# A causal mask moved from TensorE to GpSimd in an attention and mixture-of-experts kernel

## The chip, the cores and the metric

The kernel runs on one core of a Trainium2 chip. The metric is device time in microseconds (us) of one execution. Engines are named as in the profile: PE is TensorE's matmul, PEld its weight load, DVE is VectorE, ACT is ScalarE, POOL is GpSimd, SP is the engine that issues most DMAs. L679 means line 679 of the kernel before.

## The reference, cut to what matters

The input x has 8 sequences of 1024 tokens with 512 features. The first half is attention with 16 heads of 32 features on the normalized x. Queries and keys are the cosine and sine of angles, 64 numbers per head. The part that the change touches is the causal mask:

```python
scores = jnp.einsum('bqhd,bkhd->bhqk', Q, K) / scale
causal = jnp.triu(jnp.ones((S, S), dtype=bool), k=1)
scores = jnp.where(causal, -jnp.inf, scores)
attn = jax.nn.softmax(scores, axis=-1)
out = jnp.einsum('bhqk,bkhd->bqhd', attn, V).reshape(B, S, D)
```

The second half is a mixture of experts: a router picks two of 8 experts for each token, each expert takes at most 160 tokens of a sequence, and tokens go through two matrix products (512 to 2048 to 512). Both halves are added to x.

## The kernel before

**Stages.** The first 1275 us or so are attention; the rest is the experts, which the change leaves alone. Attention runs in 32 *chunks*: chunk n is sequence n // 4 and features 128 (n % 4) onwards, that is four heads. A chunk has two *pairs* of heads, and each pair two *halves* of 512 queries. Only what is not wholly masked is computed: half 0 has 3 score tiles, half 1 has 7. The last three tiles of each half hold the keys on the diagonal; the helper `tiles_of` makes them out of one key block with 512 queries, two blocks with 384 and 128 queries side by side, and one block with 256. Call them tiles a, b and c of the half: a has one diagonal square of 128 keys by 128 queries, b two, c one. So a half has 4 such squares, a chunk 16, the kernel 512.

**A score tile.** `scores` (L670) multiplies keys by queries into PSUM (L679): for each of the two heads of the pair one matmul that uses 64 of the 128 rows of the array, so two run side by side, and each shows as two passes in the trace. In tiles a, b and c four bf16 matmuls follow into the same PSUM tile (L693), which add a large negative number where a key is later than its query; `keys_b` and `later_b` are the constants they multiply. Then ACT takes the exponential into the SBUF tile `e` (L699). PSUM holds three such tiles of two banks. `attend` (L713) multiplies the weights `e` by the values into `av`; DVE scales it into `av_sb` (L721). `turn` transposes `av_sb` (L215), divides by the sum of the weights (L748, L750) and puts the result into `o_p`.

**Beside it.** For the next chunks DVE and ACT make the angles of queries and keys (`qk_pre` L520, `angle` L440, squares L444, sines L447 and L589, products L450) and of the values (`v_pre` L621, L626; `v_post`). The base of an angle (position times a constant) is made once per feature chunk by `make_base` (L463 to L493) and read back later. From the fifth chunk on, the *router* of the sequence before runs in steps between these: `features` transposes two token tiles and copies them (L832), `next_rows` normalizes the next two (L807) and stores them to DRAM, `sums` multiplies by the router's weights (L869), copies the products (L874), gathers them (L852) and adds the bias into `prob` (L876). Most of these steps fall into the chunks with n % 4 == 1.

**Order.** PE, ACT, DVE and SP run in the order in which the program text issues the work; the loop over n writes this order out by hand, with generators (`some`, `with_asides`, `route_on`) that advance one tile at a time. In pair 0 the 10 score tiles come first (5, then 5 with other work between), then all its products with the values; in pair 1 the three tiles of half 0, two of half 1, then the products of half 0. A half's products therefore stand some tiles behind its exponentials. POOL is placed by a scheduler and executes what it gets in order: a few constants, the scatters of tokens to slots (L764, 16 for each sequence, each behind the one before), the fetch of the slots back (L991), the gathers of the experts (L1080), and, near the end of attention, a few subtractions of weights (L1159). Scatters of a sequence are issued together, in the last chunk of the next sequence.

Of the kernel before, what the change touches and what calls it, by code (L numbers as in the profile page):

```python
# [63 lines left out]

FIRST = 6 * P
REACH = [(0, -(-FIRST // CAP)), (FIRST // CAP, B)]

FAR = 1000.0 * math.sqrt(2 * DH) / (UNIT * UNIT)

ROOT_GUESS = float(0x5F3759DF)  # L70

# [2 lines left out]
def preln_attn_moe_kernel(  # L74
# [184 lines left out]
    nc.gpsimd.memset(ones, 1.0)  # L259

    before = own.tile([P, P], F32, name="before")


    keys_b = own.tile([P, 2, P], BF16, name="keys_b")
    nc.gpsimd.memset(keys_b, 0.0)
    later_b = own.tile([P, 2, P], BF16, name="later_b")
    e_row = own.tile([P, E], F32, name="e_row")
    e_row_low = own.tile([P, E], F32, name="e_row_low")
    dropped = own.tile([P, NTT, TOPK], F32, name="dropped")
# [12 lines left out]
    empty = own.tile([P, E * CAP // P, 2], I32, name="empty")  # L282
    nc.vector.memset(empty, 0)

    later = row2.tile([P, NCH, 2 * P], F32, name="xT", bufs=1)[:, :3, :P]

    def mask():
        for part in range(2):
            for a in range(2):
                r = slice(a * 64, (a + 1) * 64)  # L290
                nc.gpsimd.tensor_copy(later_b[r, part, :], later[r, 1 + part - a, :])
                nc.gpsimd.tensor_copy(keys_b[r, part, part * 64 : part * 64 + 64], ident[r, r])

    def rest_of_loads():

        nc.gpsimd.memset(later, 0.0)
        for i in range(3):
            nc.gpsimd.affine_select(
                out=later[:, i, :], in_=later[:, i, :], compare_op=ALU.is_ge, fill=-FAR,
                base=64 * (1 - i), pattern=[[1, P]], channel_multiplier=-1,  # L300
            )
# [153 lines left out]
    def make_base(c):  # L455
# [33 lines left out]
                )  # L489
        else:  # L490
            nc.vector.tensor_scalar(p, p, UNITS, None, ALU.mult)
            wrap(p, r)
        nc.sync.dma_start(base_d[c], p)  # L493
        bases[c] = p

# [173 lines left out]

    def scores(pair, h, es):  # L670

        for parts in tiles_of(h):
            n = sum(w for _, _, w, _ in parts)
            ps = two_banks()
            own_keys = parts[0][0] >= 4 * h
            for kb, q0, w, at in parts:
                for a in range(2):
                    r = slice(a * 64, (a + 1) * 64)
                    nc.tensor.matmul(  # L679
                        ps[:, a, at : at + w], lhsT=pair[r, 1, kb * P : (kb + 1) * P],  # L680
                        rhs=pair[r, 0, q0 : q0 + w], start=at == 0, stop=not own_keys,
                        skip_group_check=True,
                    )
            if own_keys:

                for part, w in ((0, 64), (1, P)):
                    for a in range(2):
                        r = slice(a * 64, (a + 1) * 64)
                        out_, late = ps[:, a, :w], later_b[r, part, :w]
                        if len(parts) == 2:  # L690
                            out_ = ps[:, a, :].rearrange("p (k q) -> p k q", q=P)[:, ::3, :w]
                            late = late.unsqueeze(1).to_broadcast([64, 2, w])
                        nc.tensor.matmul(  # L693
                            out_, lhsT=keys_b[r, part, :], rhs=late,
                            start=False, stop=part == 1, skip_group_check=True,
                        )

            e = ep.tile([P, 2, n], F32, name=f"e_{n}", bufs=8 if n == 512 else 2)
            nc.scalar.activation(  # L699
                e, ps[:, :, :n], AF.Exp, scale=UNIT * UNIT / math.sqrt(2 * DH)  # L700
            )
            es.append(e)
            yield

# [48 lines left out]
        )  # L753


    scatters = []
    scattered = {b: [] for b in range(B)}
    mixed = []

    def scatter(count=2 * NTT * TOPK, together=False):  # L760

        for _ in range(min(count, len(scatters))):
# [6 lines left out]
            if together:  # L769
# [6 lines left out]
                )  # L776
                for other in scattered[b]:
                    tc.declare_no_dep(ins, other, reason="rows of their own")
            scattered[b].append(ins)

    def router(b):
# [103 lines left out]
        for g in range(NTT // 2):  # L885
            xT = features(g)
            if last and g == 0:
                yield
            if g + 1 < NTT // 2:
                if not last:  # L890
                    yield
                next_rows(g)
            yield
            lg = sums(g, xT, lg)
            yield
# [442 lines left out]
    next(base0)  # L1338
    next(base1)
    rest_of_loads()  # L1340
    mask()
    first_stats(2, NTT)
    layernorm_first()
    rest(base0)
# [12 lines left out]
    for n in range(NCK):  # L1357
# [59 lines left out]
        else:  # L1417
            with_asides(5)
        rest(residual)
        for _ in range(3):  # L1420
            route_on(1)
        rest(angles)
        if begin:
# [5 lines left out]
        if late:  # L1429
            some(4, *products)  # L1430
        route_on(1)
        with_asides(5)
        if begin:
            square(v_st[0])
        for g in asides:
            rest(g)
        if n == 0:
            load_base(2)
            magnitude(inv_o)
        if late:  # L1440
            turn(1, halves1, pos)
            o_st = o_pre(n - 1, pos)
# [4 lines left out]
        if c == 3 and b > 0:  # L1447
            next(route)
            if b > 1:
                fetch_slots(b - 2)  # L1450
            if b < B - 1:
                scatter()


        some(3, *products)
        if more:
            qk_st = place[0]
            qk_sin(qk_st)
# [112 lines left out]
```

## Time and profile before

| | us |
|---|---|
| three timed runs | 3272.74, 3274.41, 3276.23 (median 3274.41) |
| the profiled execution | 3277.64 |
| its span, first to last instruction | 3275.9 |
| busy over the span: PE, DVE, ACT, POOL | 3190.8, 2255.8, 1323.3, 426.2 |
| attention, 35 to 1275: PE, DVE, ACT, POOL busy | 1205.69, 976.08, 1016.67, 169.47 |
| the bf16 matmuls of the mask (L693), 1536 of them: busy | 175.5 |

A PE matmul's row in the profile starts when the matmul is issued, and its end is modelled; matmuls overlap, so what one costs is read from the start of one to the start of the next, and not from its duration. A timeline row has its start, its length, engine, line, operation, the tiles it writes and reads, shapes, how many instructions were merged, and in brackets how long the engine was idle before and what ended that.

### The profile page before, as it was taken

How to read it: one execution, taken by the hardware profiler on the slowest of the kernel's cores; microseconds unless marked ns; L12 is line 12 of the kernel's file. 1: busy time of each engine (PE TensorE's matmuls, PEld its weight loads, DVE VectorE, ACT ScalarE, POOL GpSimd, SP SyncE). 2: the span in 40 equal slices, each digit the busy share in tenths (PEclk: the TensorE clock that was granted, in tenths of full speed). 3: DMA queues.
4: the chain of work that ended last, by engine and by line, in shares of the span. 5: the costliest groups of instructions: out<-in, count | busy, mean ns of one | idle time of the engine just before them, and what ended most of it. 6: DMA issues, size and time to landing. Idle time of an engine off the chain costs nothing.

```text
span 3275.9 us, 48751 instructions
## 1 busy us (share of the span) xinstructions
PE 3190.8 (97%) x18942; PEld 2164.6 (66%) x18942; DVE 2255.8 (69%) x4961; ACT 1323.3 (40%) x1617; POOL 426.2 (13%) x387
## 2 busy tenths in 40 slices
PE   5999999999999999999999999999999999999998
PEld 2444444444444444588688688688688688688687
DVE  8887888878788675755755855855855855855854
ACT  7888887878787874201201201201201201201201
POOL 3000202011110213311011011011011011011010
PEclk9999999999999999999999999999999999999999
DMA  5435454453645352322322322322322322322321
GB/s 162 143 97 166 133 147 139 132 155 104 181 114 158 91 162 70 114 54 73 103 46 73 103 46 73 103 47 72 103 48 71 104 48 69 106 49 69 105 42 26
DMA packets 235254, 319.74 MB, mean 98 GB/s; under 512 B 22456, under 2 KB 155280, under 8 KB 222992
## 3 DMA queue, kind: packets, MB, share of 16 engines
q1 hardware_dynamic: 211664, 273.38, 28.6%
q0 software_dynamic: 22912, 43.22, 7.4%
q8 instruction: 150, 2.46, 0.3%
q14 instruction: 80, 0.66, 0.1%
q10 hardware_dynamic: 448, 0.02, 0.0%
HBM read 187.62 MB, written 61.82 MB: 76 GB/s over the span
## 4 chain that ended last, share of the span: by engine, by line
PE 57%; DVE 0%; DMA 0%; issue 0%; POOLq 0%; POOL 0%; DVEq 0%
PE ps_p L1220 29%; PE ps_p L1175 27%; PE ps_t L1121 1%; DMA slots<-slot_d 0%; DMA out_dram<-y,slots 0%; DVE w L1053 0%; DVE w_t L1054 0%; DVE w_t L1052 0%; DVE w_t L1055 0%; POOLq L1567 0%; POOL slot_d L764 0%; POOL slots L991 0%; DVE y L1236 0%; DVE p L1257 0%; DVE p L1258 0%
## 5 line engine op out<-in xcount | busy, mean ns | idle before, releaser
L699 ACT ACTIVATE e<-ps_s 128x1024 f32<-128x1024 f32 (+1 forms) x640 | 569.7, 938 | 202.5 <-PE ps_s L679 113.6
L679 PE MATMUL ps_s<-qk 64*128 64x512 f32 (+3 forms) x3072 | 601.9, 507 | 40.3 <-DMA qk<-qk_r 12.4
L1220 PE MATMUL ps_p<-w,hid 128*128 128x256 f32 x2560 | 567.1, 379 | 0.0
L1220 PEld LDWEIGHTS ps_p<-w,hid 128*128 128x128 f32 x2560 | 484.0, 190 | 66.6 <-DVE hid L1193 0.5
L713 PE MATMUL av<-e,v 128*64 128x512 f32 (+3 forms) x3072 | 524.7, 491 | 0.0
L1220 PE MATMUL ps_p<-w_t,hid 128*128 128x256 f32 x1920 | 430.5, 379 | 2.0 <-DVE w_t L1054 2.0
L679 PEld LDWEIGHTS ps_s<-qk 64*128 64x128 f32 x3072 | 262.0, 188 | 231.4 <-issue 111.7
L1220 PEld LDWEIGHTS ps_p<-w_t,hid 128*128 128x128 f32 x1920 | 361.1, 190 | 50.1 <-DVE w_t L1054 2.8
L713 PEld LDWEIGHTS av<-e,v 128*64 128x64 f32 x3072 | 200.8, 137 | 284.7 <-issue 268.1
L1175 PE MATMUL ps_p<-xe,w 128*128 128x256 f32 (+1 forms) x1024 | 297.8, 434 | 0.0
L1175 PE MATMUL ps_p<-xe_s,t 128*128 128x256 f32 (+1 forms) x1024 | 296.9, 433 | 0.0
L1175 PE MATMUL ps_p<-xe,t 128*128 128x256 f32 (+1 forms) x1024 | 296.8, 433 | 0.0
L764 POOL DMA_INDIRECT slot_d<-token,slot x128 | 162.4, 1268 | 974.3 <-issue 627.4
L1251 ACT COPY p<-ps_p 128x256 f32<-128x256 f32 x40 | 14.7, 369 | 604.3 <-PE ps_p L1220 604.3
L1175 PEld LDWEIGHTS ps_p<-xe,t 128*128 128x128 f32 x1024 | 194.4, 190 | 80.9 <-issue 0.4
L1175 PEld LDWEIGHTS ps_p<-xe_s,t 128*128 128x128 f32 x1024 | 194.3, 190 | 80.7 <-issue 0.4
L1175 PEld LDWEIGHTS ps_p<-xe,w 128*128 128x128 f32 x1024 | 193.4, 190 | 80.8 <-DVE hid L1193 3.5
L1080 POOL DMA_INDIRECT xg<-xn_d,source x76 | 75.2, 990 | 1074.8 <-PE ps_t L1121 1064.0
L1242 POOL DMA_INDIRECT out_dram<-y,slots x80 | 126.5, 1582 | 624.1 <-DVE y L1237 624.1
L1190 ACT ACTIVATE p<-ps_p,b_t 128x256 f32<-128x256 f32 (+1 forms) x128 | 65.5, 511 | 336.2 <-PE ps_p L1175 182.1
L1207 ACT ACTIVATE hid<-hid,b_more 128x256 f32<-128x256 f32 (+1 forms) x128 | 71.8, 561 | 274.8 <-DVE hid L1206 270.0
L1194 ACT ACTIVATE hid<-hid 128x256 f32<-128x256 f32 (+1 forms) x128 | 60.1, 470 | 299.5 <-DVE hid L1193 295.3
(224 smaller groups left out, 3818.6 us busy)
## 6 DMA issues: line engine op xcount, KB each, us to landing
w<-in_L_ffn_W_dram SPq DMA_DIRECT2D x256, 256.0 KB
w<-in_L_ffn_W_dram SPq DMA_DIRECT2D x64, 512.0 KB
qk<-qk_c SPq DMA_DIRECT2D x124, 256.0 KB
qk<-qk_r SPq DMA_DIRECT2D x124, 256.0 KB
qk_base<-base_d SPq DMA_DIRECT2D x28, 1024.0 KB
xn_d<-xn SPq DMA_DIRECT2D x72, 256.0 KB
x_mid<-in_L_attn_x_dram SPq DMA_DIRECT2D x16, 1024.0 KB
out_dram<-x_mid SPq DMA_DIRECT2D x8, 2048.0 KB
```

The costliest lines, as they stand in the source:

```text
L679: nc.tensor.matmul(ps[:, a, at : at + w], lhsT=pair[r, 1, kb * P : (kb + 1) * P], rhs=pair[r, 0, q0 : q0 + w], start=at == 0, stop=not own ...
L699: nc.scalar.activation(e, ps[:, :, :n], AF.Exp, scale=UNIT * UNIT / math.sqrt(2 * DH))
L713: nc.tensor.matmul(av[a * 64 : (a + 1) * 64, q0 - 512 * h :], lhsT=vt[:, kb, 2 * pr + a, :], rhs=es[i][:, a, at : at + w], start=kb == 0, ...
L764: queued = nc.gpsimd.indirect_dma_start(out=slot_d[b], out_offset=bass.IndirectOffsetOnAxis(ap=idx, axis=0), in_=src, in_offset=None,)
L1080: ins = nc.gpsimd.indirect_dma_start(out=xg, out_offset=None, in_=xn2_d[i % 2], in_offset=bass.IndirectOffsetOnAxis(ap=source[:, e, j0 + j ...
L1121: nc.tensor.transpose(ps[:, c, :], xg[:, c * P : (c + 1) * P], ident)
L1175: nc.tensor.matmul(ps, lhsT=weights[:, k, :], rhs=rows[:, k, :], start=k == 0, stop=k == 1)
L1190: nc.scalar.activation(p1, product(b11, a11), AF.Identity, bias=b1_t[:, e * NHC + q : e * NHC + q + 1])
L1194: nc.scalar.activation(h11, h11, AF.Relu)
L1207: nc.scalar.activation(h12, h12, AF.Relu, bias=more)
L1220: nc.tensor.matmul(ps, lhsT=hs[k][:, part, cols], rhs=ws[k][weight], start=k == 0, stop=k == NHQ - 1,)
L1242: ins = nc.gpsimd.indirect_dma_start(out=out, out_offset=bass.IndirectOffsetOnAxis(ap=meta[:, e, jj[r], 0:1], axis=0), in_=ys[r], in_offse ...
```

## The change

It has four parts.

1. **The mask.** The bf16 matmuls, their constants and the code that makes them go. After the exponential of a tile a, b or c, POOL runs one `affine_select` for each diagonal square: 128 keys by 2 heads by 128 queries of `e` are kept where the query is not earlier than the key, and set to zero elsewhere. These 512 instructions are kept in program order on POOL.
2. **The scatters.** They are no longer issued together: after the last tile of each half, two of those that wait are issued, in program order, so that 16 take eight halves. Those of sequence 6 are held back for the ending, where they also were before.
3. **The router.** In group 1, `sums` comes ahead of `next_rows`, and one step of the router is issued later in the chunk, so that the group's `sums` and then its rows stand behind the values' angles.
4. **The third base.** `make_base(2)` is issued in three steps through chunk 0 rather than in one, and the small preparation of `inv_o`, by which `av_sb` is scaled, comes ahead of it.

```diff
-    keys_b = own.tile([P, 2, P], BF16, name="keys_b")
-    nc.gpsimd.memset(keys_b, 0.0)
-    later_b = own.tile([P, 2, P], BF16, name="later_b")
...
-    def mask():
-        for part in range(2):
-            for a in range(2):
-                r = slice(a * 64, (a + 1) * 64)
-                nc.gpsimd.tensor_copy(later_b[r, part, :], later[r, 1 + part - a, :])
-                nc.gpsimd.tensor_copy(keys_b[r, part, part * 64 : part * 64 + 64], ident[r, r])
...
             nc.vector.tensor_scalar(p, p, UNITS, None, ALU.mult)
-            wrap(p, r)
+            if c == 2:
+                yield
+                nc.vector.tensor_scalar(r, p, ROUNDT, ROUNDT, ALU.add, ALU.subtract)
+                yield
+                nc.vector.tensor_tensor(p, p, r, ALU.subtract)
+            else:
+                wrap(p, r)
...
-                        rhs=pair[r, 0, q0 : q0 + w], start=at == 0, stop=not own_keys,
+                        rhs=pair[r, 0, q0 : q0 + w], start=at == 0, stop=True,
                         skip_group_check=True,
                     )
-            if own_keys:
-
-                for part, w in ((0, 64), (1, P)):
-                    for a in range(2):
-                        r = slice(a * 64, (a + 1) * 64)
-                        out_, late = ps[:, a, :w], later_b[r, part, :w]
...
-                        nc.tensor.matmul(
-                            out_, lhsT=keys_b[r, part, :], rhs=late,
-                            start=False, stop=part == 1, skip_group_check=True,
-                        )
 
             e = ep.tile([P, 2, n], F32, name=f"e_{n}", bufs=8 if n == 512 else 2)
             nc.scalar.activation(
                 e, ps[:, :, :n], AF.Exp, scale=UNIT * UNIT / math.sqrt(2 * DH)
             )
+            if own_keys:
+
+                for _, _, _, at in parts:
+                    own_ = e[:, :, at : at + P]
+                    tc.keep_in_program_order(
+                        nc.gpsimd.affine_select(
+                            out=own_, in_=own_, compare_op=ALU.is_ge, fill=0.0, base=0,
+                            pattern=[[0, 2], [1, P]], channel_multiplier=-1,
+                        )
+                    )
+            if parts is tiles[-1] and not hold[0]:
+
+                scatter(2)
             es.append(e)
             yield
...
+            if g == 1 and not last:
+
+                yield
+                lg = sums(g, xT, lg)
+                yield
+                next_rows(g)
+                yield
+                continue
...
         rest(residual)
-        for _ in range(3):
+        for _ in range(2):
             route_on(1)
         rest(angles)
...
             some(4, *products)
         route_on(1)
+        route_on(1)
         with_asides(5)
...
         if n == 0:
-            load_base(2)
             magnitude(inv_o)
+            base2 = make_base(2)
+            next(base2)
...
-            if b < B - 1:
-                scatter()
+            hold[0] = b == B - 1
 
 
         some(3, *products)
+        if n == 0:
+            next(base2)
...
+        if n == 0:
+            some(NTT, *products)
+            rest(base2)
```

More of the change, by code (lines that the diff above doesn't have):

```diff
@@ L66 @@
 REACH = [(0, -(-FIRST // CAP)), (FIRST // CAP, B)]
-FAR = 1000.0 * math.sqrt(2 * DH) / (UNIT * UNIT)
 ROOT_GUESS = float(0x5F3759DF)
@@ L283, in preln_attn_moe_kernel @@
     nc.vector.memset(empty, 0)
-    later = row2.tile([P, NCH, 2 * P], F32, name="xT", bufs=1)[:, :3, :P]
-    def mask():
-        for part in range(2):
-            for a in range(2):
-                r = slice(a * 64, (a + 1) * 64)
-                nc.gpsimd.tensor_copy(later_b[r, part, :], later[r, 1 + part - a, :])
-                nc.gpsimd.tensor_copy(keys_b[r, part, part * 64 : part * 64 + 64], ident[r, r])
-    def rest_of_loads():
[L296 to L300, printed above, removed]
-            )
+    def rest_of_loads():
         nc.gpsimd.affine_select(
@@ L670, in scores @@
     def scores(pair, h, es):
-        for parts in tiles_of(h):
+        tiles = tiles_of(h)
+        for parts in tiles:
             n = sum(w for _, _, w, _ in parts)
@@ L680, in scores @@
                         ps[:, a, at : at + w], lhsT=pair[r, 1, kb * P : (kb + 1) * P],
-                        rhs=pair[r, 0, q0 : q0 + w], start=at == 0, stop=not own_keys,
+                        rhs=pair[r, 0, q0 : q0 + w], start=at == 0, stop=True,
                         skip_group_check=True,
                     )
-            if own_keys:
-                for part, w in ((0, 64), (1, P)):
-                    for a in range(2):
-                        r = slice(a * 64, (a + 1) * 64)
-                        out_, late = ps[:, a, :w], later_b[r, part, :w]
[L690 to L693, printed above, removed]
-                            out_, lhsT=keys_b[r, part, :], rhs=late,
-                            start=False, stop=part == 1, skip_group_check=True,
-                        )
             e = ep.tile([P, 2, n], F32, name=f"e_{n}", bufs=8 if n == 512 else 2)
@@ L753, in turn @@
         )
-    scatters = []
+    scatters, hold = [], [False]
     scattered = {b: [] for b in range(B)}
@@ L778, in scatter @@
                     tc.declare_no_dep(ins, other, reason="rows of their own")
+            else:
+                tc.keep_in_program_order(queued)
             scattered[b].append(ins)
@@ L1340, in preln_attn_moe_kernel @@
     rest_of_loads()
-    mask()
     first_stats(2, NTT)
```

## The prediction

> **What bounds the kernel now.** The change touches attention alone, so I took the 1240 us of it first. By stretches of one chunk each, PE is busy nearly always in an ordinary chunk, and ACT and DVE are close behind; a chunk with router steps is longer and PE has pauses in it:
>
> ```profile
> 577.78:614.17 36.39, 36.34 (x306) 17.92 (x304) 30.69 (x69) 32.14 (x33) 0.00 (x0) 1.00 0.43 116
> 686.50:731.23 44.73, 42.10 (x434) 21.12 (x436) 33.21 (x50) 34.40 (x34) 4.67 (x5) 1.00 0.68 208
> ```
>
> Columns: stretch, its length, then PE, PEld, DVE, ACT and POOL busy, clock, DMA. Busy PE could hide waiting, so next PE's timeline, start against start, over tiles a, b, c of one half:
>
> ```profile
> 607.91 0.60 PE L679 MATMUL ps_s<-qk 64*128 64x512 f32 x2
> 608.35 0.25 PE L693 MATMUL ps_s<-later_b,keys_b 64*128 64x64 bf16 x4
> 608.43 1.09 PE L679 MATMUL ps_s<-qk 64*128 64x384 f32 x8
> 609.35 0.33 PE L693 MATMUL ps_s<-later_b,keys_b 64*128 64x128 bf16 x4
> 609.52 0.60 PE L679 MATMUL ps_s<-qk 64*128 64x256 f32 x4
> 609.95 0.25 PE L693 MATMUL ps_s<-later_b,keys_b 64*128 64x64 bf16 x4
> 610.13 1.08 PE L713 MATMUL av<-e,v 128*64 128x512 f32 x4
> ```
>
> No bracket stands here: PE issues without a wait, and 607.91 to 608.35 is the price of a 512-column pass, 0.43. So PE is the bound of ordinary chunks by what it issues, and the mask is part of that. The third view is ACT's timeline over the same chunk, for who is next:
>
> ```profile
> 606.90 4.39 ACT L699 ACTIVATE e<-ps_s 128x1024 f32<-128x1024 f32 x5 [2.50 <-PE ps_s L679]
> 611.62 2.19 ACT L444 ACTIVATE qk_f<-qk_f,split_c 128x1024 f32<-128x1024 uint16 x2 [0.33 <-DVE qk_r L440]
> 614.17 4.47 ACT L699 ACTIVATE e<-ps_s 128x1024 f32<-128x1024 f32 x5 [0.36 <-PE ps_s L693]
> ...
> 621.79 4.39 ACT L699 ACTIVATE e<-ps_s 128x1024 f32<-128x1024 f32 x5 [0.23 <-PE ps_s L679]
> ...
> 634.66 2.75 ACT L699 ACTIVATE e<-ps_s 128x1024 f32<-128x1024 f32 x3 [0.17 <-PE ps_s L693]
> ```
>
> Once a chunk ACT waits 2.50 for PE, while PE does products of values, which hold no mask. Between two such waits it idles only 0.33 + 0.36 + 0.23 + 0.17 = 1.09 of 35.9 us.
>
> **The mask leaves PE.** Starts give 0.08 for tile a (608.35 to 608.43), 0.17 for b, and for c again 0.08 (its 0.18 holds 0.10 of a change of matmul shape, which stays). That is 0.33 a half, 1.33 a chunk with four halves, 43 us in 32 chunks. It may be more: the tile from 608.43 to 609.35 takes 0.92, where two passes of 512 columns are 0.86; 0.06 behind a mask, twice a half, make it 0.45 a half and 58 us. I take 0.33 and keep 0.45 for the range.
>
> What is late next is ACT: an ordinary chunk can shrink by at most the 1.09 that ACT idles. DVE takes more (below), so I take 0.8 for 24 ordinary chunks: 19 us. In the 8 chunks with n % 4 = 1 ACT idles 10 us (34.40 of 44.73), so all 1.33 comes out: 11 us.
>
> **The selects on POOL.** Prices of such work:
>
> ```profile
> L298 POOL TENSOR_SCALAR_AFFINE_SELECT xT<-xT 128x128 f32<-128x128 f32 x3 | 0.8, 284 | 0.0
> L1159 POOL TENSOR_TENSOR t<-w,t 128x256 f32<-128x256 f32 x12 | 9.0, 748 | 0.5
> ```
>
> A square is 128x256. Twice 284 ns is 0.57 us, less if part of the 284 does not grow: memsets of 128 and 384 elements took 195 and 410 ns, 0.84 ns for each further one, so 284 + 128 x 0.84 = 0.39. Bounds are 0.28 and 0.75; I take 0.4, 6.4 us a chunk on an engine that is busy 169 of 1240. It is free if each select ends before the products that read it. The tightest place is half 0 of pair 1. Its exponentials start at 634.66; a ends at 635.7, b at 636.8, c at 637.4. These follow:
>
> ```profile
> 637.15 2.28 DVE L450 SCALAR_TENSOR_TENSOR qk_r<-qk_f,qk_r 128x2048 f32<-128x2048 f32 x1
> 639.24 1.08 PE L713 MATMUL av<-e,v 128*64 128x512 f32 x4
> ```
>
> Tile a is read at 639.24, b 0.86 later, c at 640.96. With 0.4 each, a is done at 636.1, b at 637.6, c at 638.0: 3 us early. If c must sit out the DVE instruction, it is done at 640.3 or so, still early. In chunks with n % 4 = 0 this place has up to 1 us less; all other tiles have 4 to 15 us between exponential and product, but for chunk 0.
>
> Do POOL and DVE hold each other up? Yes, where the trace has both:
>
> ```profile
> 51.83 2.79 DVE L491 TENSOR_SCALAR qk_base<-qk_base 128x2048 f32<-128x2048 f32 x1
> 54.66 1.23 DVE L225 TENSOR_SCALAR x_mid<-qk_base 128x2048 f32<-128x2048 f32 x1
> ...
> 1316.17 1.02 DVE L807 TENSOR_SCALAR xn<-x_mid,mv,rstd 128x512 f32<-128x512 f32 x1 [0.28 <-PE ps_t L823]
> ```
>
> The first ran beside POOL's iota (51.22 to 53.55) and took 2.79, where one as large alone took 1.23; the last ran beside a POOL subtraction and took 1.02, against a median of 0.54. How a select meets a DVE instruction with two operands in SBUF no row shows. The Trainium skill, "SBUF — State Buffer", section "Who interferes with whom", speaks against this change: a DVE instruction with two SBUF inputs and a GpSimd one that reads SBUF exclude each other for their whole length. By it DVE's products, sums and shifts, some 14 of 36 us a chunk, would be closed to selects and the other way round; estimated, four tenths of the 6.4 us of selects, 2.5 us, would stop DVE in each chunk, and if all of that were on the path, the ordinary chunks would give nothing and the sum below would be 16 and not 35.
>
> My bounds: nothing, or 16 x 0.4 = 6.4 us a chunk if every select stops DVE. DVE is busy 30.7 of 36.4, so the upper end eats all its idle time. I take what sits on the path: the product at 637.15 held up by b's two selects (up to 0.8), the shift L440 by one (up to 0.4), 0 to 1.2 in all, half of it 0.6. This reaches ACT by the wait "0.33 <-DVE qk_r L440". About half is late there: this is the 0.3 by which I took 0.8 and not 1.09.
>
> **The router's order.** In a router chunk, DVE's two normalizations wait for earlier stores, the values' angles follow, and PE waits behind all of them for a PSUM bank:
>
> ```profile
> 695.43 0.55 DVE L807 TENSOR_SCALAR xn<-x_mid,mv,rstd 128x512 f32<-128x512 f32 x1 [0.85 <-DMA xn_d<-xn]
> ...
> 700.07 0.17 DVE L876 TENSOR_TENSOR prob<-ps_s,br_b 128x16 f32<-128x16 f32 x1
> ```
>
> ```profile
> 700.29 1.14 PE L679 MATMUL ps_s<-qk 64*128 64x384 f32 x8 [0.79 <-DVE prob L876]
> ```
>
> With the two rows moved behind, prob comes 2 x 0.55 + 0.25 + 0.85 = 2.2 earlier, and this wait goes; the rows fall into 2.4 us in which DVE idles after 700.24, and their two stores have until the next transposes. The wait is there in four of the seven router chunks, 0.8, 1.1, 0.8 and 2.2: 5 us. Bounds 0 and 9 (all waits of PE for prob).
>
> **The third base.** In chunk 0 the transposes wait 1.49 and 2.40 for `av_sb`, which stands behind the whole base on DVE; both go, 3.9. Against it, POOL's iota for the fourth base waits for a store until 51.22 and then stands in front of the selects of half 1, whose exponentials end at 53.3 to 54.7; with the DVE instructions above they come some 1.5 to 2 late. Net 2 us (0 to 4).
>
> **The scatters.** Issue to issue is 2.4 to 5.7, so two hold POOL for about 5 us after the last tile of a half; the next select is due 6 to 10 us later. After the last pair of a sequence the fetch waits for landings too (34.2 us in 7 waits) and takes 1.6: 11 to 14 us in all, in a router chunk, from 703.2 to about 716, where selects must be done by 718.6 to 720.4. I take 2 us for six sequences (0 to 12). The constants no longer made at the start, 4 us of POOL before 17.4, stood before an idle time of 13.7: nothing.
>
> **Sum.** 19 + 11 + 5 + 2 - 2 = 35. From the profiled execution's 3277.6 this is 3242.6; the median of the three runs is 3.2 lower, so 3239, and I say 3240.
>
> **Rivals.**
> - *PE gets all of it*, because ACT's path shortens with PE's: 58 + 5 + 4 = 67, so 3207 to 3222. For it: ACT's 2.50 is spare. Against: PE already waits 0.2 for an exponential at the end of a chunk. 0.14.
> - *DVE is held up by the selects* nearly as far as its idle time allows, and ordinary chunks give 0.2: 24 x 0.2 + 8 x 0.7 + 5 = 15, about 3259 (3252 to 3268). For it: the rows of 1316 and 51.83. 0.20.
> - *The selects come too late* and the wait at PSUM becomes one at the products: slower. From 635.7 to 640.96 there are 5.3 us for four selects. At 0.75 each with two stops of 2.28 they need 7.5, 2.2 too late, in 31 chunks 68; less the 35, about 3307. It decides from 5.3 + 35 / 31 = 6.4 us on. Against: 0.75 is the price of two inputs. 0.13.
> - *No change* by more than 0.2%, 6.5 us, which is about what a measurement of this kernel can tell: all freed time comes back as waits for ACT. 0.07.
>
> The forecast, 3224 to 3252, has 0.46. Faster by over 0.2% are it and the first two rivals, 0.80; same 0.07; slower 0.13. The range goes from 3206, where PE gets all, to 3274, so that it leaves out the slower case and little else.
>
> **What would show it.** Ordinary chunks near 35.1 us instead of 35.9 to 36.4. PE starts of b's scores 0.86 after a's, with no L693. ACT's small waits near zero and its 2.50 still there: the step on ACT is right. If instead the 2.50 shrinks, PE got more. POOL selects of 0.4 us; over 0.7 they speak for the slower rival, and so do waits of the products for POOL. DVE's two-operand products above 2.28 us on the mean show the hold-up. The wait for prob at the first place is gone. I am wrong if PE waits for POOL in ordinary chunks, or if chunks don't shrink while PE idles.

## The result, and the profile after

The changed kernel is slower: its seven runs took 3282.36 to 3288.77 us, median 3285.71, against 3276.23 for seven runs of the kernel before. The ratio is 1.0032, 95% interval 1.0023 to 1.0042, so 9.5 us were lost where 35 were expected to be won. On another chip it was 3287.82 against 3269.19, ratio 1.0059 (1.0045 to 1.0073). The profiled execution took 3288.23 with a span of 3286.5. What was lost lies in attention: its last exponential ends at 1286.2 instead of 1275.4, while the rest takes 2000.3 instead of 2000.5.

By chunk (from the start of a chunk's first exponential to that of the next, read from the two traces) the difference of 10.8 comes together like this:

| chunks | before | after | difference of the sum |
|---|---|---|---|
| 0 and 1 | 40.90, 38.04 | 44.48, 42.20 | +7.7 |
| n % 4 = 0, seven | 36.2 to 36.8 | 37.6 to 37.8 | +8.6 |
| n % 4 = 1, seven | 43.7 to 47.3 | 44.3 to 45.2 | -2.8 |
| n % 4 = 2, eight | 36.4 to 37.1 | 36.7 to 38.1 | +4.4 |
| n % 4 = 3, seven | 35.9 to 36.7 | 36.2 | +0.4 |
| the last, and the start | 43.0 | 36.0 | -7.5 |

So ordinary chunks did not shrink; most of them grew. The stretches of chunks 14 and 17 (stretch, length, then PE, PEld, DVE, ACT and POOL busy, clock, DMA) in the changed kernel:

```profile
590.04:626.92 36.88, 35.43 (x258) 16.48 (x256) 32.19 (x71) 31.52 (x33) 9.18 (x16) 1.00 0.45 122
700.72:745.31 44.59, 40.75 (x386) 19.69 (x388) 33.73 (x51) 34.13 (x35) 17.40 (x24) 1.00 0.69 207
```

PE lost 0.91 us of busy time in the ordinary chunk (36.34 before), and the chunk is 0.49 longer: PE, without a pause before, now has pauses. DVE has 1.5 us more. ACT's timeline of chunk 15 says where the pauses begin:

```profile
634.37 4.26 ACT L671 ACTIVATE e<-ps_s 128x1024 f32<-128x1024 f32 x5 [0.27 <-PE ps_s L664]
...
643.65 1.99 ACT L425 ACTIVATE t_r<-t_r 128x1024 f32<-128x1024 int32 x2
647.05 1.28 ACT L671 ACT_TABLE_LOAD   x1 [1.42 <-PE ps_s L664]
648.35 2.48 ACT L671 ACTIVATE e<-ps_s 128x1024 f32<-128x1024 f32 x3
...
656.29 4.26 ACT L671 ACTIVATE e<-ps_s 128x1024 f32<-128x1024 f32 x5 [2.60 <-PE ps_s L664]
```

After the last sine ACT needs another table for the exponential of pair 1's first tile. The load takes 1.28 us, and here it *waits for PE's scores* and only then runs. In the kernel before the load followed the sine at once, and the exponential (634.66, in the prediction) waited 0.17:

```profile
633.21 1.28 ACT L699 ACT_TABLE_LOAD   x1
```

So 1.28 us that lay beside PE's work are now between PE's scores and their exponential, and PE, which needs the PSUM bank back, stands still. PE's timeline of the changed kernel:

```profile
647.64 0.66 PE L213 MATMUL ps_s<-ident,av_sb 64*128 64x64 f32 x16
649.43 0.70 PE L664 MATMUL ps_s<-qk 64*128 64x256 f32 x4 [1.13 <-ACT e L671]
```

The tables of waits over attention have both ends of it (engine, line that waited, what it waited for; sum, times, longest). In the kernel before:

```profile
ACT L699 <- PE ps_s L693: 4.9, 1, 4.9
PE ps_s L679 <- ACT e L699: 5.0, 10, 1.4
```

In the changed kernel:

```profile
ACT L671 <- PE ps_s L664: 60.9, 32, 4.6
PE ps_s L664 <- ACT e L671: 49.1, 68, 2.9
```

The first row of each is the load itself: this instruction, which reads no data of the program, waited once and now waits in each of 32 chunks. The built program shows why. A buffer of `e` that is used again was last written by ACT, and is now last written by POOL. So the exponential has two waits, one for PE and one for POOL, and in the program the one for PE hangs on the table load in front of it:

```
before   t_r (sine) | LoadActFuncSet              | Activation e [waits PE]
after    t_r (sine) | LoadActFuncSet [waits PE]   | Activation e [waits Pool]
```

In the traces, too, the semaphore on which the exponential at 634.66 waits in the kernel before is waited for right ahead of the load in the changed kernel (at 647.01), and the exponential at 648.35 waits on another.

The selects themselves, duration minimum, median and maximum in ns over attention (two of the 512 lie outside; the count at the end is of a sample):

```profile
L679 POOL TENSOR_SCALAR_AFFINE_SELECT e<-e x510: 396/406/2451, 38.7 to 1285.8; 128x256 f32<-128x256 f32 x170
```

Most take the 0.4 us that were reckoned, but some six times as long. Here are two of them, 2.34 and 0.40 long, and the product of DVE that began 0.2 before the first:

```profile
183.51 2.70 POOL L679 TENSOR_SCALAR_AFFINE_SELECT e<-e 128x256 f32<-128x256 f32 x2 [10.11 <-ACT e L671]
183.31 2.28 DVE L428 SCALAR_TENSOR_TENSOR qk_r<-qk_f,qk_r 128x2048 f32<-128x2048 f32 x1
```

### The profile page after: what moved, and what is told of

It reads as the page before. It is cut to its first block, busy times and chain, and to the rows that moved or that the text cites. A ratio compares the mean times of both kernels' runs of the same rounds, so it can differ in the third digit from the quotient of the medians.

```text
span 3286.5 us, 46266 instructions
## 1 busy us (share of the span) xinstructions
PE 3157.4 (96%) x17406; PEld 2118.1 (64%) x17406; DVE 2272.2 (69%) x4961; ACT 1307.4 (40%) x1617; POOL 716.6 (22%) x886
## 4 chain that ended last, share of the span: by engine, by line
PE 85%; DVE 8%; ACT 3%; POOL 1%; DMA 1%; issue 1%; SPq 0%; POOLq 0%; DVEq 0%; ACTq 0%
PE ps_p L1215 29%; PE ps_p L1170 29%; PE av L698 13%; PE ps_s L664 11%; ACT e L671 2%; PE ps_s L213 2%; POOL e L679 1%; DVE qk_f L504 1%; PE ps_t L1116 1%; DVE v L428 0%; DVE xT L819 0%; DMA base_d<-x_mid 0%; DVE av_sb L706 0%; DVE v_p L605 0%; DVE v_p L610 0%
## 5 line engine op out<-in xcount | busy, mean ns | idle before, releaser
L664 PE MATMUL ps_s<-qk 64*128 64x512 f32 (+3 forms) x3072 | 569.0, 503 | 78.7 <-ACT e L671 49.1
L671 ACT ACTIVATE e<-ps_s 128x1024 f32<-128x1024 f32 (+1 forms) x640 | 555.5, 943 | 173.7 <-PE ps_s L664 172.0
L679 POOL TENSOR_SCALAR_AFFINE_SELECT e<-e 128x256 f32<-128x256 f32 x512 | 308.1, 628 | 630.9 <-ACT e L671 629.5
L749 POOL DMA_INDIRECT slot_d<-token,slot x128 | 151.5, 1184 | 165.5 <-DMA slot_d<-token,slot 135.7
```

Of the source, the lines that this page charges most:

```text
L664: nc.tensor.matmul(ps[:, a, at : at + w], lhsT=pair[r, 1, kb * P : (kb + 1) * P], rhs=pair[r, 0, q0 : q0 + w], start=at == 0, stop=True, s ...
L671: nc.scalar.activation(e, ps[:, :, :n], AF.Exp, scale=UNIT * UNIT / math.sqrt(2 * DH))
L679: nc.gpsimd.affine_select(out=own_, in_=own_, compare_op=ALU.is_ge, fill=0.0, base=0, pattern=[[0, 2], [1, P]], channel_multiplier=-1,)
L749: queued = nc.gpsimd.indirect_dma_start(out=slot_d[b], out_offset=bass.IndirectOffsetOnAxis(ap=idx, axis=0), in_=src, in_offset=None,)
```

## The experiments

T1 is the theory that the late table load ate the gain; T2, the rival, that POOL's selects and ACT bound the chunks, so that without the late load there would be another wait. One thing is needed to read the numbers: the kernel before took 3263 to 3277 us depending on the chip, while a kernel with selects that ran on two chips differed by 1 to 4 us between them. So times of runs are mostly set against each other where before took the same (3263.8, 3262.8 and 3263.4 on three chips), and a ratio is to before on the same chip.

**The table load.** One exponential of one element, right behind the last sine, for the load to hang on:

```diff
         if late:
             sine(o_st[1])
+        nc.scalar.activation(warm, split_c, AF.Exp)
```

> The changed kernel with one more instruction on ScalarE: an exponential of one element right after a chunk's last sine, so that the load of the exponential's table (1.28 us) hangs on an instruction that waits for nothing. Theory T1 (the table load, pushed behind the wait for the scores because the exponential now also waits for POOL, is what ate the gain): PE's wait of 1.30 us behind the first tile of pair 1 goes in 32 chunks, 41 us less, 0.2 x 32 = 6 us of ScalarE added at most partly: about 3246 where the changed kernel is 3286, so 0.9% below the kernel before. Rival T2 (POOL's selects and ScalarE bound the chunks, the table load only stands where a wait would be anyway): the wait moves to another place and the time stays at 3275 or above.

Measured: 3254.97, ratio 0.9976 (0.9967 to 0.9985), and once more on another chip:

> The run with the early table load once more, as the yardstick of this call: the kernel before took 3263.8 us on the one chip and 3276.6 on the other, while runs with selects hardly moved (3255, 3258), so ratios of different calls can't be set against each other. Expected: 3255 to 3258 whatever the kernel before takes.

Measured: 3256.17, ratio 0.9978 (0.9969 to 0.9988). The timeline of ACT has the load back behind the sine, without a wait:

```profile
624.34 1.99 ACT L425 ACTIVATE t_r<-t_r 128x1024 f32<-128x1024 int32 x2
626.34 1.28 ACT L1459 ACT_TABLE_LOAD   x1
627.63 0.20 ACT L1459 ACTIVATE warm<-split_c 128x1 f32<-128x1 f32 x1
627.76 2.48 ACT L671 ACTIVATE e<-ps_s 128x1024 f32<-128x1024 f32 x3
```

For the size of it the changed kernel ran again, on a chip where before took 3269.19:

> The changed kernel once more, unaltered, for the price of the late table load: 3285.7 stood on a chip where the kernel before takes 3276, the runs with the early load (3255 and 3256) on chips where it takes 3263. If this chip takes 3263 for before: T1's price by the spans of the traces (3286.5 less 3252.8) is 34 us, so 3285 to 3290; by the ratios of the calls (1.0032 less 0.9977) it is 18, so 3274.

Measured: 3287.82. So it stays at 3286 to 3288 and the early load is worth some 32 us (3287.8 less 3256.2, on two chips; the ends of attention differ by 30.1 in these two traces and by 36.5 in the first two). By the ratios to before it would be 18 to 27, since before differs between the chips. T2 has fallen for this part, and PE waits 19.5 us for exponentials instead of 49.1:

```profile
PE ps_s L664 <- ACT e L671: 19.5, 45, 2.5
```

The opposite experiment makes the load late in the kernel before, where no select exists:

```diff
+            if h == 0 and parts[0][0] == 0 and pair is pairs[1]:
+                nc.scalar.activation(warm, ps[:, 1, w - 1 : w], AF.Square)
             e = ep.tile([P, 2, n], F32, name=f"e_{n}", bufs=8 if n == 512 else 2)
```

> The kernel before with one more instruction on ScalarE: a square of one column that reads the first scores of pair 1 ahead of their exponential, so that the table load stands behind the wait for PE, with no select anywhere. T1: the 1.30 us of PE's wait appears in 32 chunks, 35 to 45 us: about 3315. T2: ScalarE has the room, at most 0.3 us a chunk: 3286 or less.

Measured: 3298.08, ratio 1.0108 (1.0092 to 1.0123), 34.3 us slower. Its ACT timeline:

```profile
648.53 0.17 ACT L699 ACTIVATE warm<-ps_s 128x1 f32<-128x1 f32 x1 [1.47 <-PE ps_s L693]
648.70 1.28 ACT L701 ACT_TABLE_LOAD   x1
```

T1 is shown from both sides: 32 and 34 us, where 41 (32 times 1.28) was expected. That the missing fifth fell into time that was idle anyway is likely, but not shown.

**What the mask is worth on PE, and what the selects cost.** The selects are left out:

```diff
-            if own_keys:
+            if False:
```

> The changed kernel without the selects: the causal mask inside the diagonal squares is left out of the computation; the rest stays. It bounds what the mask's leaving PE can be worth. Both T1 and T2 expect the waits of PE for POOL and the late table load to go: 3276 less 43 (PE) + 5 (router) + some = about 3232. What tells them apart is its distance to e1: T1 (table load first, selects nearly free) wants e1 within 15 us of this run; T2 (selects hold DVE and PE up) wants e1 over 35 us above it. If this run itself is above 3260, then neither: PE's mask was not on the path.

Measured: 3229.19, ratio 0.9896 (0.9881 to 0.9911). Chunks take 35.3, 42.6, 35.6 and 34.9 for n % 4 = 0 to 3. The table load follows the sine at once here, so this run has no added exponential. With 3255 for the run with the early load the selects cost some 26 us, between what T1 and T2 wanted: T1 is the larger part, but the selects are not free. Next, with the early load, the selects work on the same data, for nobody:

```diff
-                            out=own_, in_=own_, compare_op=ALU.is_ge, fill=0.0, base=0,
+                            out=aside, in_=own_, compare_op=ALU.is_ge, fill=0.0, base=0,
```

> The run with the early table load, but the selects write their squares to a tile of their own that nobody reads: the causal mask inside the diagonal squares is left out of the computation, POOL does all of its work, and no product waits for it. It splits the 26 us (3255 less 3229) that the selects still cost there. Theory L (lateness: products wait for selects): near 3232, as without selects. Rival D (the selects slow DVE, and the late shift and squares that follow make PE wait): near 3252, as with them. My estimate: DVE's busy time was 25.6 us larger with selects (2280.4 against 2254.8), so mostly D: 3248.

Measured: 3252.31, ratio 0.9926 (0.9912 to 0.9939), on a chip where before takes 3276.6. This alone was inconclusive: by ratios lateness is the larger part, by chunk lengths it is DVE. Beside the run with the early load, on one chip:

> The run with the selects on squares that nobody reads (the causal mask inside the diagonal squares left out), beside its yardstick on one chip. The traces say that chunks 4 to 30 took 1023.7 us with it, 1024.2 with the real selects and 1004.2 without any, and chunks 0 and 1 79.9 against 82.4 and 78.2. So theory D (selects hold up DVE) wants it 3 to 6 us below the yardstick; theory L (products wait for selects), to which the ratios of the two calls pointed (0.9926 against 0.9976), wants it 15 us below.

Measured: 3248.09, ratio 0.9954 (0.9941 to 0.9968). It is 8 us below the run with real selects (3256.2) and 19 above the one without (3229.2): lateness 8, DVE held up 19. The 8 is loose. In the traces attention ends at 1250.2 with real selects, at 1245.9 with these and at 1226.1 without any, so lateness is 4 there and the rest 20; the other 5 us between the first two spans lie in the experts, where no select runs. So lateness is 4 to 8, and theory D has the larger part. That the 19 goes through DVE is by exclusion so far: in this trace neither an exponential nor a product with the values waits for POOL.

**How DVE's 0.8 us a chunk reach PE.** In an ordinary chunk of the run with the early load, qk_r's product starts at 629.93 and takes 2.39, so it ends at 632.32, but DVE's shift into the same buffer has to wait until its stores have landed:

```profile
624.97 2.28 DVE L428 SCALAR_TENSOR_TENSOR qk_c<-qk_f,qk_c 128x2048 f32<-128x2048 f32 x1
629.93 2.39 DVE L428 SCALAR_TENSOR_TENSOR qk_r<-qk_f,qk_r 128x2048 f32<-128x2048 f32 x1
...
639.90 1.23 DVE L418 TENSOR_SCALAR qk_r<-qk_f 128x2048 int32<-128x2048 int32 x1 [2.36 <-DMA qk<-qk_r]
```

ACT's squares wait for the shift, and PE for the exponentials behind them:

```profile
641.16 2.19 ACT L422 ACTIVATE qk_f<-qk_f,split_c 128x1024 f32<-128x1024 uint16 x2 [1.19 <-DVE qk_r L418]
```

To test this chain, sine, product and stores of qk_r go first:

```diff
-        nc.scalar.activation(c, c, AF.Sin, bias=quarter_c, scale=-STEP_ACT)
+        sine(r)
         for _ in between:
             pass
-        sine(r)
+        nc.scalar.activation(c, c, AF.Sin, bias=quarter_c, scale=-STEP_ACT)
...
-        for i, t in enumerate((st[0], st[2].bitcast(F32))):
+        for i, t in ((1, st[2].bitcast(F32)), (0, st[0])):
```

> The early table load with real selects (3256 where the kernel before takes 3263), and one change of order: the sines, and the product and the stores of qk_r, go ahead of those of qk_c. Without selects the run takes 3229, with selects that nobody reads 3248, so 19 us come from POOL's selects holding DVE up. The trace of one ordinary chunk says how: qk_c's product ends 0.75 us later, its four stores hold SP's queue, qk_r's stores land 0.76 later, the shift that writes qk_r again waits for them (2.36 us), ScalarE's squares wait for the shift (1.19), and PE for the exponentials behind (0.77). If that chain is the 19 us, the new order takes the stores off the path: 3240 (3236 to 3246). Rival: DVE is simply short of time with its 0.8 us more a chunk, and the wait moves to the next thing it does: 3253 or more.

Measured: 3242.22, ratio 0.9937 (0.9924 to 0.9951). The shift follows what is in front of it at once:

```profile
616.02 2.28 DVE L428 SCALAR_TENSOR_TENSOR qk_r<-qk_f,qk_r 128x2048 f32<-128x2048 f32 x1
622.15 2.39 DVE L428 SCALAR_TENSOR_TENSOR qk_c<-qk_f,qk_c 128x2048 f32<-128x2048 f32 x1
...
629.68 1.22 DVE L418 TENSOR_SCALAR qk_r<-qk_f 128x2048 int32<-128x2048 int32 x1
```

ACT's waits for the shift fall from 21.9 us to 3.1 (chunks 4 to 30), and chunks with n % 4 = 3 take 34.92, as without selects (34.89), though DVE is as much held up as ever (2280.7 us busy in all; 2280.4 without the new order). The controls:

> The same order without selects (the causal mask inside the diagonal squares left out), the control: how much the order is worth where nothing holds DVE up. Without it ScalarE waits 8.9 us for the shift in all and PE 15.4 for exponentials: 3229 becomes 3222 to 3229. If it falls as much as the run with selects does, the order has nothing to do with the selects.

Measured: 3224.36, ratio 0.9881 (0.9866 to 0.9897), 5 us less than without the new order.

> The kernel before with the router's order (0.9987 of before) and the new order of sines and stores; mask on PE, no selects. There PE bounds the ordinary chunks, and ScalarE's wait for the shift is 0.3 to 1.8 us in some: 3260 becomes 3255 to 3260. If it comes below 3245, the mask should have stayed on PE.

Measured: 3256.80, ratio 0.9978 (0.9969 to 0.9987), 3 us less. With selects the order is worth 14, without them 3 to 5. So it takes back 9 to 11 of the 27 us that the selects cost (3256.2 less 3229.2), and by the waits above that is the chain by the stores. What selects still cost beside the control, 18 us, lateness included, stands in the chunks with n % 4 = 0 (0.6 each) and 1 (0.4 each), in chunks 0 and 1 together (2.5), in chunk 30 (2.8) and in chunk 16 (4.0: PE waits 1.92 for a select there and then has half its clock for 3.4 us). These waits were not traced further. The added exponential, which the runs without selects do not have, is no large part of it: chunks with n % 4 = 2 and 3 take 35.61 and 34.92 with it and 35.55 and 34.86 without.

**Half the mask on each engine.** The bf16 products stay for the tile with two diagonal squares, or, in a second run, for the two tiles with one; the rest is selected:

```diff
+            by_pe = own_keys and parts[0][0] - 4 * h in (1,)
+            if by_pe:
                 for part, w in ((0, 64), (1, P)):
...
-            if own_keys:
+            if own_keys and not by_pe:
```

(The second run has `(0, 2)` in place of `(1,)`.)

> The early table load, and the mask of the tiles with two diagonal squares back on PE as bf16 products, so that half of the selects go. By the prediction's prices PE gets 0.17 us a half back, 0.67 a chunk, 21 us if all of it is on the path; selects cost 20 us in 27 chunks, so half of them 10 to 13. If both prices are linear: 3255 + 12 (PE, by 1029.4 less 1004.2 for the whole mask) - 12 = 3255. If each engine has some slack of its own, half a load on each costs less than half: 3245. Above 3260 would speak for PE's price alone.

Measured: 3251.18, ratio 0.9960 (0.9946 to 0.9973).

> The other half: the mask of the two tiles with one diagonal square is back on PE (0.16 us a half, 0.65 a chunk), the tile with two squares keeps its selects. The last tile of a half then has no select between its exponential and its product, where PE waited 0.5 to 0.8 in every fourth chunk (8 chunks, 5 us). Linear prices: 3255 + 12 - 12 - 5 = 3250; with slack on each engine 3240.

Measured: 3253.11, ratio 0.9968 (0.9956 to 0.9980). Both are 3 to 5 us below the full set of selects (3256.2), which is hardly more than the noise, since the intervals of the ratios overlap; they are nearer to linear prices than to slack. With qk_r first:

> Half the mask on PE (the tile with two squares), early table load (3251 where the kernel before takes 3263), and the new order. If the chain by the stores is what half the selects still cost, 3241; if PE is the bound there, 3248 or more.

Measured: 3242.30, ratio 0.9934 (0.9920 to 0.9947): the same as with all selects, so the two remedies do not add up.

> The best version so far (early table load, qk_r first: 3242) with one tile a chunk masked by PE again: the last tile of the first half of pair 1, whose select ends 0.5 us behind the product that reads it in every fourth chunk. PE gets 0.08 to 0.18 us a chunk back, 3 to 6 us; chunks with n % 4 = 0 lose 0.6 (36.01 to 35.4), 7 of them 4.5 us, and those with n % 4 = 1 up to 0.4. If lateness of that select is what these chunks still wait for, they go to 35.5 and the time is 3239; if PE's 0.18 is on the path in all chunks, 3243 or more.

Measured: 3244.68, ratio 0.9923 (0.9910 to 0.9937). Chunks with n % 4 = 0 stay at 35.9 to 36.3. PE's wait of 0.36 for the select of that tile is gone, and one of 0.2 to 0.6 at the next transposes has come in its place. So the first branch has fallen. The second is not shown by the time: chunks with n % 4 = 2 and 3 take 35.61 and 34.92, with PE's 0.18 or without it, and in the trace attention ends 4.7 us earlier than with all selects (1234.4 against 1239.1) while the experts, which the edit leaves alone, are longer (2008.5 against 2001.4).

**The smaller parts of the change.** The router's order alone, on the kernel before (the `g == 1` branch and the moved `route_on` of part 3, nothing else):

> The kernel before with the router's order alone (two rows behind the values' places and the sums). By the prediction's step 5 us less, bounds 0 and 9: 3271 where the kernel before is 3276; the wait of PE for prob at the first place goes. Rival: the wait only moves to the next bank, 3276.

Measured: 3260.01, ratio 0.9987 (0.9978 to 0.9996), 3.8 us less. PE's waits for `prob` over attention from chunk 4 on fall from 9.0 us to 4.5, the longest from 2.2 to 0.6. With the third base in three steps added:

> The kernel before with the router's order and the third base in three steps, no selects. By the prediction the transposes' waits for av_sb in chunk 0 go, 3.9 us less than with the router's order alone (whose chunks 0 and 1 took 41.48 and 37.73): 75.3 for both, and 3256 on a chip where the kernel before takes 3264. Rival: DVE is late for the same work at the next step, so both chunks together stay at 78 to 79 and the time at 3260.

Measured: 3273.73, ratio 0.9994 (0.9985 to 1.0003). The base gains nothing that shows. The transposes' waits for `av_sb`, 3.9 us before, are gone, but PE then waits 6.2 us for exponentials in the same two chunks, which take 80.3 together (79.2 with the router alone).

The fourth base's iota, behind the selects of chunk 0 (with the early load):

```diff
-            nc.gpsimd.iota(
+            (tc.keep_in_program_order if c > 2 else (lambda it: it))(nc.gpsimd.iota(
```

> The run with the early table load, and the iota of the fourth base (POOL, 2.3 us, behind a wait of 7.8 us for a store) kept where the program has it, behind the selects of chunk 0. Chunks 0 and 1 took 41.19 and 41.17 us against 40.60 and 37.57 without selects. If the iota in front of the selects is what makes these chunks long, they come to 40.6 and 38 and the time falls by 3 to 4 us (3251, ratio 0.9965); if it is the selects' meeting with DVE's two bases, they stay and the time is 3255.

Measured: 3258.26, ratio 0.9948 (0.9934 to 0.9961; before took 3276.6 there). Chunk 0 falls to 39.93 and chunk 1 grows to 43.03, 83.0 together against 82.4. PE's wait for selects in chunk 0 falls from 2.38 to 0.71, but its waits for exponentials behind do not shrink: 1.38 becomes 3.62 in chunk 0, and 2.41 and 2.55 become one of 5.05 in chunk 1. The iota is not what makes these chunks long. With qk_r first they take 77.4, and there ACT's wait of 3.05 for the shift, with PE's 2.41 behind it, is gone.

The scatters as before, not in twos and without a place kept among the selects (the call that kept it is taken out as well):

```diff
-            if parts is tiles[-1] and not hold[0]:
-                scatter(2)
...
+            if b < B - 1:
+                scatter()
```

> The run with the early table load, but the scatters handed out as in the kernel before, all of a sequence's at a chunk's end and without a place kept on POOL. By the prediction the scatters in twos cost 2 us for six sequences (0 to 12) since selects stand behind them; undone in this manner 32 scatters stand before the selects at once, so worse: POOL needs about 5 us for two of them, 80 us for 32 on the whole, and products wait for selects behind them: 3270 or above against 3255. Rival: the scheduler puts the scatters beside the selects and the time is 3253 or less, so the twos themselves cost.

Measured: 3498.88, ratio 1.0684 (1.0669 to 1.0699). Six chunks, those with n % 4 = 3 from chunk 7 on, take 76 to 79 us, and PE stands still for 39 to 42 in each. The POOL timeline of one shows the end of the row of scatters, each waiting for the one before to land, and the selects behind them:

```profile
365.71 0.97 POOL L746 DMA_INDIRECT slot_d<-token,slot  x1 [1.40 <-DMA slot_d<-token,slot]
368.09 0.97 POOL L746 DMA_INDIRECT slot_d<-token,slot  x1 [1.41 <-DMA slot_d<-token,slot]
369.08 1.48 POOL L679 TENSOR_SCALAR_AFFINE_SELECT e<-e 128x256 f32<-128x256 f32 x4
```

So with selects behind them the scatters cannot stand in one row; whether twos gain or cost anything by themselves was not run.

## Why the prediction was wrong, point by point

The steps from run to run, beginning where before takes 3264: router -4, mask off PE -31 (3260.0 to 3229.2, with the scatters in twos and the third base), selects' lateness +8, DVE held up +19, late table load +32, together +24, which is 3288. Each step is the difference of two runs, so that they meet the changed kernel's time is no proof of its own. The first chip's before was 13 us slower, so there the loss was 9.5.

- **"The mask leaves PE", 0.33 a half, capped by what ACT idles: right.** Predicted 19 + 11 = 30, measured 31. Against the kernel with the router's order, ordinary chunks shrink by 0.8 to 1.0 without selects, router chunks by 0.9 instead of 1.33 (and only seven of the eight have router steps). PE was the bound, as the timeline said.
- **"What is late next is ACT": right in kind, wrong in what it left out.** This is the step that failed. It took ACT's gap of 0.17 at 634.66 as fixed and asked only how far the scores could move up. The selects were held to be free if each ends before the products that read it; that the exponential which fills the buffer again must wait for the select too was put at nothing. That wait was short, but it pushed the wait for PE onto the instruction in front, and the load ran late. The table load at 633.21 stood in the same timeline, hidden by the merged rows that were quoted. No rival had this mechanism; the slower rival (3307, selects too late) was on the right side of before for another reason. Price: some 32 us.
- **"The selects on POOL", 0.4 each: right** for most (minimum 0.396, median 0.406), but the mean is 0.63, since 68 of 512 take over 1 us.
- **"3 us early", so hidden: mostly right.** Real selects cost 4 to 8 us more than selects that nobody reads. The place named, half 0 of pair 1, is where products wait in chunks with n % 4 = 0: 0.36 us with the early load, 0.7 in the changed kernel. It is tighter than reckoned, since one of the selects there takes 2.34 us (next point).
- **"Do POOL and DVE hold each other up", 0.3 a chunk: far too small.** This is the term that was mis-sized: it is 19 us, about 0.6 a chunk. DVE's busy time grows by 25.6 us (2280.4 with selects, 2254.8 without), 0.8 a chunk, near the 0.6 that was reckoned for the path; but "about half is late there" took one wait of ACT from a row of before, and the stores in between, which make the shift late, were not followed. The Trainium skill, "SBUF — State Buffer", section "Who interferes with whom", says that whoever comes second waits for the whole instruction. The trace of the changed kernel agrees for POOL: 47 of the 68 long selects lie mainly beside one of DVE's products L428, and in 30 of the 32 chunks one that starts 0.2 after qk_r's product takes 2.33 to 2.35, as at 183.51. So where the prediction let a select hold the product up, the product mostly held up the select. For DVE it is far milder: with the early load its largest product takes 2.33 on the mean against 2.28 without selects. More was added to each of the shifts L418 of 2048 elements (1.30 against 1.23) and the normalizations L392 (0.63 against 0.55), which have one input; the prediction had counted shifts among the instructions with two. The same section says that one-input forms can take part too, if they run in a mode with two ports; the runs do not show which mode they ran in.
- **The router's order, 5 us: right** (3.8, interval 1.3 to 7.2).
- **The third base, 2 us: nothing that shows.** The 3.9 went, and came back behind exponentials. The counter-cost, selects behind the fourth base's iota, is there (PE waits 4.42 for them in chunk 0 of the changed kernel, 2.38 with the early load), but with the iota behind the selects the chunks are no shorter.
- **The scatters, 2 us:** not measured alone. That they cannot stand in one row in front of selects is shown.
- **The chances.** "Slower" had 0.13, all of it for selects that come too late. In the sum of 35 no term stood for what a new wait can do on ACT.

The prediction's own test, ordinary chunks near 35.1, was met only when the selects were out (34.9 to 35.6), and nearly met with the early load and qk_r first: 36.0, 43.0, 35.6, 34.9. That version, at 0.9937 of before, beats both kernels, as do its two variants with part of the mask on PE; 3242 to 3245 for all three, too close to rank.

## What to carry to other kernels

When an instruction gets a second wait, look at what the built program does with both: a wait can land on a table load, or whatever stands in front, and put its time behind the data. Give such a load an instruction of its own, without waits, at the place where it should run.

When an engine that is not the bound gets slower, follow its output through buffers and stores: here 0.8 us of DVE a chunk cost PE time because one buffer could not be written again before its stores had landed, and taking one of two products first, with its stores, took back 9 to 11 of the 27 us that the selects cost. Compare kernels on one chip: the kernel before itself moved by more between chips (13 us) than the change did.

## What the runs showed that was not expected

With the mask on PE the last chunk has two lengths: 43.0 us in the trace of the kernel before and 43.1 in the run with the third base, both on chips where before takes 3276, and 36.4 in the run with the router's order alone, where it takes 3264. The stretches of that chunk in the kernel before and in the run with the router's order, columns as above:

```profile
1232.41:1275.43 43.02, 37.83 (x304) 18.12 (x302) 19.74 (x37) 22.78 (x24) 12.24 (x15) 0.92 0.05 11
```

```profile
1218.93:1255.35 36.42, 35.06 (x304) 17.62 (x302) 19.65 (x37) 22.55 (x24) 12.27 (x15) 1.00 0.06 13
```

In the first PE stands still for 2.25 and 1.52 us around 1260 and is granted half the clock from 1262.02 on, for 6.8 us (mean 0.92):

```profile
1261.28 1.39 PE L679 MATMUL ps_s<-qk 64*128 64x512 f32 x4 [2.25 <-issue]
1264.19 2.08 PE L679 MATMUL ps_s<-qk 64*128 64x512 f32 x4 [1.52 <-DVE o_p L750]
```

The same comes with PE's wait of 4.42 for POOL's selects in chunk 0 of the changed kernel:

```profile
55.49:62.32 6.83, 5.79 (x20) 2.46 (x22) 1.94 (x3) 5.08 (x4) 2.06 (x4) 0.50 0.00 0
```

The clock is 0.50 over these 6.83 us, which is 3.4 us of PE's work lost. So a wait of PE of a few us can cost most of its length a second time. It need not: waits of 2.20 (kernel before, 855.42) and 1.92 (qk_r first, 660.81) were followed by 3.4 us at half the clock, one of 3.10 (qk_r first, chunk 0) by none. The experts, whose code is the same in all runs, took 2000 to 2009 us in the traces of runs with the whole mask, in part for the same reason: the clock is nowhere halved in them in the kernel before (2000.5), and for 10.2 us in the second trace of the changed kernel (2006.9). By these traces the last chunk is about half of the 13 us by which the kernel before differs between chips; the rest stays open.
